# A weighted neighbour sum in a two-layer graph kernel: each partition holds eight list edges in a row, summed on VectorE for two destinations ahead of the one-hot products

## The chip, the cores and the metric

One Trainium2 chip; the kernel uses one of its cores. The metric is device time in microseconds of one execution. Ten executions of the kernel before gave a median of 6719.75 us (6715.77 to 6725.78). The profile and the trace come from one further execution.

## The reference, cut to what matters

6250 nodes with 256 features and 206,250 edges, sorted by destination (100,000 random pairs in both directions and a self-loop for each node; the sources are in random order). Two layers. The first is a graph attention and a routed FFN. The second is a weighted neighbour sum with two dense products and a dense mixture-of-experts FFN, gated by a second graph attention over another edge list:

```python
x = x + _L0_gnn_ref(_layernorm(x, axis=-1), edge_index, ...)
x = x + _L0_ffn_ref(_layernorm(x, axis=-1)[None], ...)[0]
x = x + _L1_gnn_ref(_layernorm(x, axis=-1), src, dst, edge_weight, L1_gnn_W1, L1_gnn_b1, L1_gnn_W2, L1_gnn_b2)
x = x + _L1_ffn_ref(_layernorm(x, axis=-1)[None], ...)[0]

def _L1_gnn_ref(embeddings, edge_src, edge_dst, edge_val, W1, b1, W2, b2):
    ego_emb = embeddings @ W1.T + b1
    messages = edge_val[:, None] * embeddings[edge_src]
    neighbor_emb = jax.ops.segment_sum(messages, edge_dst, num_segments=embeddings.shape[0])
    interaction_emb = neighbor_emb * embeddings
    side_emb = (neighbor_emb + interaction_emb) @ W2.T + b2
    out = ego_emb + side_emb
    out = jnp.where(out >= 0, out, LEAKY_SLOPE * out)
    norm = jnp.sqrt(jnp.sum(out * out, axis=1, keepdims=True))
    return out / jnp.maximum(norm, EPS)

# the second FFN, for each of its four experts
    g = jnp.where(topk_i == ei, w, 0.0).sum(-1)
    hh = jax.nn.gelu(x @ W1[ei] + b1[ei], approximate=False)
    out = out + g[..., None] * (hh @ W2[ei] + b2[ei])
```

The change is in the neighbour sum, `messages` and `segment_sum`.

## The kernel before, in words

The node features X stay in SBUF as 49 blocks of 128 nodes. The stages follow one another:

| stage | us in the trace | what it does |
|---|---|---|
| start | 0 to 97 | check of the edge list (check_stream, L982), list columns loaded and turned into the partitions (turn_rows, L1050) |
| layer 0 attention | 97 to 2250 | layer norm, projection, stream of the edges |
| layer 0 FFN (ffn0, L651) | 2250 to 3306 | routed FFN on TensorE in tiles; beside it a generator (sorted_edges, L1381) sorts the second edge list, a few steps per tile |
| gates, layer norm | 3306 to 3401 | the outputs of the routed FFN are gated (L631), the table tab_ef of normalised rows is written |
| neighbour sum ("n1f", L1793) | 3402 to 5644 | the stage that the change rewrites |
| layer 1 attention and gating (layer1_fast) | 5644 to 6718 | stream of the second edge list; y of the experts is read, gated and added (put, L1656) |

The neighbour sum goes over the edges in 202 pieces of Q = 8 columns of 128 edges. A column of 128 edges lies across the partitions: partition p of column j holds edge (8q + j) x 128 + p of the list. For each piece
- GpSimd issues eight indirect DMAs (gather, L233), each of which fetches the 128 source rows of a column from tab_ef into g1 (five buffers);
- ScalarE multiplies each column by its edge weights (L1921);
- VectorE compares the destinations of the columns with an iota and so makes eight one-hot matrices of 128x128 (one_hots, L1092);
- TensorE multiplies each one-hot by its column (L1901; one f32 product shows as two matmul records) and adds up in PSUM, in acc. An acc stands for a window of 128 destinations and takes two pieces (16 columns).

VectorE copies a finished acc to SBUF (kept, L1906). The window is then moved onto the block of 128 nodes that it belongs to by a shift product (move, L1827). When a block's sum is whole, a chain of steps follows, one per iteration: side (L1832), dense (L1841), norm (L1852), next_ln (L1861) and next_h (L1866), which ends with the input of the second FFN for the block. When four blocks are there, start (in dense_ffn) puts the work items of their expert FFN in a list: inner (L1560: matmuls, then the gelu on ScalarE, L1565) and outer (L1571: matmuls, then the addition of the bias b2 on VectorE, L1576, and a store of y to DRAM). A call of beside() issues the matmuls of one item, and the gelu or addition of the item before it. What is left when the pieces are over is issued in a loop at the end.

The order on each engine is written out by hand (manual_schedule): in iteration s_ the gathers of piece s_ are issued, then the products of piece s_ - 3 with three calls of beside() between them, then the steps of the chain, then the scalings and one-hots of piece s_ - 2. Each engine takes its own instructions in this order.

A list is taken by this fast path if a check finds that each column's destinations lie within its window (flag, in check_stream); else a general path runs.

Of the kernel before, what the change touches and what calls it, by code (L numbers as in the profile page):

```python
# [10 lines left out]

# [8 lines left out]
F32 = mybir.dt.float32  # L20
# [50 lines left out]
def tile_kernel(ctx, tc, src_ins, out):  # L71
# [841 lines left out]


    class Stream:
# [8 lines left out]
        def __init__(self, name, edges, slack, nodes, group=None):  # L924
# [57 lines left out]
    def check_stream(s, dst, flag, last_d, dl_d, psum=None, lend=None):  # L982
# [4 lines left out]
        with ExitStack() as held:  # L987
# [34 lines left out]
            nc.sync.dma_start(last_d, t)  # L1022

# [21 lines left out]
            nc.vector.tensor_reduce(bad, v, AX.XY, OP.add)  # L1045
            ps = pp.tile([P, 4, P], F32, name="pt_s")[:, 0, 0:1]
# [26 lines left out]
    Q = 8  # L1073
# [430 lines left out]

    def layer1_weights(lp):
# [16 lines left out]
    def dense_ffn(e_pool, fp, fpp, y_d):  # L1522
# [12 lines left out]
        b2 = e_pool.tile([P, E1, D], F32, name="b2")  # L1535
        nc.scalar.dma_start(b2, I["L1_ffn_b2"][None].to_broadcast([P, E1, D]))
# [31 lines left out]
        def outer(g, e, j):  # L1568
# [22 lines left out]
    def layer1_fast(s1, si1, dl1, il1, ha_d, tab_1, y_d):  # L1591
# [3 lines left out]
        with tc.tile_pool(name="g1f", bufs=1) as g1, tc.tile_pool(name="f1w", bufs=2) as fp:  # L1595
# [12 lines left out]
            nc.vector.scalar_tensor_tensor(own, own, 0.2, own, op0=OP.mult, op1=OP.max)  # L1608
            vec = g1.tile([P, 3, D1], F32, name="vec")
# [46 lines left out]
            def put(gates, j, b):  # L1656
                y = ys.pop(b)
                for e in range(E1):
                    nc.vector.scalar_tensor_tensor(X[:, b, :], y[:, e, :], gates[:, j, e:e + 1], X[:, b, :],
                                                   op0=OP.mult, op1=OP.add)  # L1660
# [20 lines left out]
    def fast(flag_s0, last_d, dl_d):  # L1681
# [7 lines left out]
        si = kp.tile([P, C * P], I32, name="si")  # L1689
        dl = kp.tile([P, C * P], F32, name="dl")  # L1690
        wt_d = dram.tile([P, C * P], F32, name="wt_d")
        tab = dram.tile([NP, D + H0], F32, name="tab")
        with tc.tile_pool(name="gat0f", bufs=1) as g0:
            il = g0.tile([P, C * P], F32, name="il")
            NI = g0.tile([P, NT, 2 * H0], F32, name="NI")
            with tc.tile_pool(name="rows", bufs=1) as p:
# [83 lines left out]
        with tc.tile_pool(name="sort", bufs=1) as sp, tc.tile_pool(name="sort_ps", bufs=1, space=PSUM) as pp:  # L1780
            ffn0(sorted_edges(s1, sp, pp, si1, dl1, il1, flag1))
# [11 lines left out]
        with tc.tile_pool(name="n1f", bufs=1) as ep, tc.tile_pool(name="n1fw", bufs=2) as mp, \  # L1793
                tc.tile_pool(name="n1f_ps", bufs=1, space=PSUM) as pp, \
                tc.tile_pool(name="f1_ps", bufs=2, space=PSUM) as fpp:
            wt = ep.tile([P, C * P], F32, name="wt")
            nc.sync.dma_start(wt, wt_d)
# [11 lines left out]
            acc, piece, hots, ems, sums_of = {}, {}, {}, {}, {}  # L1809
            T = s0.T  # L1810
            npiece = -(-T // Q)
            stages = {}

            def span(q):
# [163 lines left out]
```

## Time and profile before

| | us |
|---|---|
| median of 10 runs | 6719.75 |
| profiled execution | 6719.51 |
| its span | 6717.7 |

Busy time of the engines in the span, and in the neighbour sum (3402 to 5500, from the first gather to the last):

| engine | whole span, us | share | 3402 to 5500, us |
|---|---|---|---|
| TensorE matmul (PE) | 4323.3 | 64% | 1711.0 |
| VectorE (DVE) | 3120.9 | 46% | 479.6 |
| ScalarE (ACT) | 1545.3 | 23% | 998.3 |
| GpSimd (POOL) | 4083.4 | 61% | 1527.2 |

The mean granted TensorE clock over the span is 0.794 of full speed. The page also shows the span in 40 slices: a digit is the busy share in tenths, PEclk is the granted clock in tenths, and DMA is the mean busy share of the 16 DMA engines.

```
PE   4466666666666569999647888888888885111111
DVE  5355555555555781443332222222222222677777
ACT  2000000000000112322124544444444441000000
POOL 0677777777777112232157777667666752777774
PEclk9677777777777679999868999999999997555555
DMA  4544554454454135556553444334333431232222
```

A slice is 168 us, so the neighbour sum is slices 21 to 33. There TensorE is the busiest, GpSimd the next, and VectorE is idle most of the time. In a row of instruction groups the columns are: line, engine, operation, output and inputs, tile shapes, count, then busy time and mean duration in ns, then the idle time before them and what ended it. In a timeline row they are: start, duration, engine, line, operation, names, shapes, count, and in brackets the idle time before it with what ended that. "issue" is time in which the engine waited for nothing that the profile shows. L12 is line 12 of the kernel.

### The profile page before, as it was taken

How to read it: one execution, taken by the hardware profiler on the slowest of the kernel's cores; microseconds unless marked ns; L12 is line 12 of the kernel's file. 1: busy time of each engine (PE TensorE's matmuls, PEld its weight loads, DVE VectorE, ACT ScalarE, POOL GpSimd, SP SyncE). 2: the span in 40 equal slices, each digit the busy share in tenths (PEclk: the TensorE clock that was granted, in tenths of full speed). 3: DMA queues.
4: the chain of work that ended last, by engine and by line, in shares of the span. 5: the costliest groups of instructions: out<-in, count | busy, mean ns of one | idle time of the engine just before them, and what ended most of it. 6: DMA issues, size and time to landing. Idle time of an engine off the chain costs nothing.

```text
span 6717.7 us, 63729 instructions
## 1 busy us (share of the span) xinstructions
PE 4323.3 (64%) x19844; PEld 3330.4 (50%) x19844; DVE 3120.9 (46%) x7430; ACT 1545.3 (23%) x3735; POOL 4083.4 (61%) x4308
## 2 busy tenths in 40 slices
PE   4466666666666569999647888888888885111111
PEld 3344444444444448888525666666666664111111
DVE  5355555555555781443332222222222222677777
ACT  2000000000000112322124544444444441000000
POOL 0677777777777112232157777667666752777774
PEclk9677777777777679999868999999999997555555
DMA  4544554454454135556553444334333431232222
GB/s 137 141 139 137 139 139 137 139 139 137 138 140 137 57 91 192 186 188 224 164 156 112 119 121 119 113 112 121 113 113 113 119 91 50 61 70 69 67 67 59
DMA packets 502118, 817.25 MB, mean 122 GB/s; under 512 B 149515, under 2 KB 322983, under 8 KB 501738
## 3 DMA queue, kind: packets, MB, share of 16 engines
q0 software_dynamic: 190688, 461.74, 25.3%
q1 hardware_dynamic: 298414, 339.67, 16.3%
q10 hardware_dynamic: 12668, 11.68, 0.6%
q8 instruction: 160, 2.62, 0.2%
q14 instruction: 188, 1.54, 0.1%
HBM read 739.86 MB, written 76.05 MB: 121 GB/s over the span
## 4 chain that ended last, share of the span: by engine, by line
PE 38%; POOL 19%; DVE 16%; issue 12%; DMA 11%; ACT 3%; DVEq 0%; SPq 0%; another core or an unknown queue 0%; POOLq 0%; ACTq 0%
POOL g L1199 16%; PE acc L1901 10%; DMA g<-tab,si 7%; PE pf L1571 5%; PE pf L1560 5%; PE ph L600 5%; PE py L613 5%; DVE oh L1092 3%; PE acc L1301 3%; DMA g<-tab_1f,si1s 2%; POOL g L233 2%; DVE g L1278 1%; PE bacc L1827 1%; PE pt L262 1%; PE ph L1738 1%
## 5 line engine op out<-in xcount | busy, mean ns | idle before, releaser
L233 POOL DMA_INDIRECT g<-tab_ef,si x1612 | 1527.2, 947 | 665.0 <-issue 553.6
L1199 POOL DMA_INDIRECT g<-tab,si x1612 | 1539.5, 955 | 492.6 <-issue 410.6
L1301 PE MATMUL acc<-g,oh 128*128 128x264 f32 x3224 | 1049.7, 491 | 332.4 <-DVE g L1278 327.4
L1901 PE MATMUL acc<-g,oh 128*128 128x256 f32 x3224 | 885.9, 418 | 422.5 <-DVE oh L1092 223.1
L1301 PEld LDWEIGHTS acc<-g,oh 128*128 128x128 f32 x3224 | 776.6, 249 | 555.3 <-DVE g L1278 387.1
L1901 PEld LDWEIGHTS acc<-g,oh 128*128 128x128 f32 x3224 | 653.0, 209 | 650.8 <-ACT g L1921 373.1
L1199 POOL DMA_INDIRECT g<-tab_1f,si1s x787 | 765.2, 972 | 247.0 <-issue 216.3
L1921 ACT ACTIVATE g<-g,wt 128x256 f32<-128x256 f32 x1612 | 676.1, 496 | 150.0 <-DMA g<-tab_ef,si 149.0
L1092 DVE TENSOR_TENSOR oh<-ips,dl 128x1024 f32<-128x1024 f32 x404 | 489.1, 1212 | 0.0
L1278 DVE TENSOR_TENSOR g<-g,pe 128x2048 f32<-128x2048 f32 (+2 forms) x301 | 487.1, 1618 | 0.0
L1301 PE MATMUL acc<-s,oh 128*128 128x72 bf16 x1267 | 96.6, 251 | 548.8 <-DVE s L1283 548.8
L1231 DVE TENSOR_TENSOR z<-g,nd 128x32 f32<-128x32 f32 (+1 forms) x301 | 59.0, 196 | 815.4 <-DMA g<-tab,si 643.4
L600 PE MATMUL ph<-xe,w 128*128 128x256 f32 x1792 | 401.2, 381 | 0.0
L1571 PE MATMUL pf<-w,h 128*128 128x256 f32 x1568 | 399.3, 402 | 0.0
L613 PE MATMUL py<-w,h 128*128 128x256 f32 x1792 | 399.2, 381 | 0.0
L1560 PE MATMUL pf<-xt,w 128*128 128x512 f32 (+1 forms) x832 | 398.3, 607 | 0.6
L576 POOL DMA_INDIRECT xg<-tab_x,gi x112 | 123.8, 1106 | 398.3 <-PE pt L585 313.4
L1301 PEld LDWEIGHTS <-oh 128*128 128x128 bf16 x1267 | 90.1, 133 | 552.6 <-issue 477.4
L600 PEld LDWEIGHTS ph<-xe,w 128*128 128x128 f32 x1792 | 340.0, 191 | 45.4
L613 PEld LDWEIGHTS py<-w,h 128*128 128x128 f32 x1792 | 337.1, 191 | 43.4
L1220 PEld LDWEIGHTS <-ot 128*128 128x128 bf16 x2879 | 116.0, 101 | 474.8 <-DVE ot L1209 422.1
L1571 PEld LDWEIGHTS pf<-w,h 128*128 128x128 f32 x1568 | 318.8, 204 | 51.2 <-issue 1.9
(461 smaller groups left out, 5062.9 us busy)
## 6 DMA issues: line engine op xcount, KB each, us to landing
w<-in_L_ffn_W SPq DMA_DIRECT2D x112, 1024.0 KB
db<-s_d SPq DMA_DIRECT2D x299, 256.0 KB
g<-tab,si POOLq DMA_INDIRECT x1612, 2.8
g<-tab_ef,si POOLq DMA_INDIRECT x1612, 2.8
y_d<-y SPq DMA_DIRECT2D x196, 128.0 KB
yb<-y_d SPq DMA_DIRECT2D x49, 512.0 KB
g<-tab_1f,si1s POOLq DMA_INDIRECT x787, 2.3
yy<-tab_y SPq DMA_DIRECT2D x7, 1792.0 KB
```

The costliest lines, as they stand in the source:

```text
L233: nc.gpsimd.indirect_dma_start(out=dst, out_offset=None, in_=table, in_offset=bass.IndirectOffsetOnAxis(ap=si[:, t:t + 1], axis=0))
L576: nc.gpsimd.indirect_dma_start(out=xg[:, i, :], out_offset=None, in_=tab_x, in_offset=bass.IndirectOffsetOnAxis(ap=gi[:, 2 * j + i:2 * j + ...
L600: nc.tensor.matmul(ph, w1[:, k, f * P:(f + 1) * P], xe[:, k, :], start=(k == 0), stop=(k == KD - 1))
L613: nc.tensor.matmul(py, hs[f][:, i * P:(i + 1) * P], w2[:, f, :], start=(f == 0), stop=(f == FC - 1))
L1092: nc.vector.tensor_tensor(o[:, :m], ips[:, None, k * P:(k + 1) * P].to_broadcast([P, m, P]), dl[:, a:a + m, None].to_broadcast([P, m, P]), ...
L1199: nc.gpsimd.indirect_dma_start(out=g[:, j, :DH + H], out_offset=None, in_=tab, in_offset=bass.IndirectOffsetOnAxis(ap=si[:, t0 + j:t0 + j ...
L1278: nc.vector.tensor_mul(gh, gh, ps[i][:, o:o + n, :, None].to_broadcast([P, n, H, CD]))
L1301: nc.tensor.matmul(acc[b].rearrange("p s w -> p (s w)"), oh[:, t - a], m_, start=(t == lo), stop=(t == hi))
L1560: nc.tensor.matmul(ph[:, :n], w1[:, e, k, f * P:(f + 1) * P], xts[g][:, k, :n], start=(k == 0), stop=(k == KD - 1))
L1571: nc.tensor.matmul(py[:, :D], hs[g, e, f][:, j * P:(j + 1) * P], w2[:, e, f, :], start=(f == 0), stop=(f == FC - 1))
L1901: nc.tensor.matmul(acc[b], oh[:, t - a], g[:, t - t0, :], start=(t == lo), stop=(t == hi))
L1921: nc.scalar.activation(piece[k][:, j, :], piece[k][:, j, :], AF.Copy, scale=wt[:, t0 + j:t0 + j + 1])
```

## The change

1. *Order of the list.* Partition p of column j of piece q holds edge (128q + p) x 8 + j: eight edges that follow one another in the list lie in one partition. Since the list is sorted, and each node has at least 15 edges, eight edges in a row have one destination or two. The check of the list gets a further condition (at most one change of destination in eight).
2. *Sums on VectorE.* Per piece the eight gathered columns are added in each partition into two sums r[0] and r[1], one for each destination of the row, with the edge weight as a scalar per partition, which is zero where the edge belongs to the other destination: two scaled copies on ScalarE and 13 multiply-and-add operations on VectorE. One comparison makes two one-hots in place of eight, and two products (four matmul records) take the place of eight (16).
3. *Lists in DRAM.* The sources, the two masked weights and the two destinations per row in the new order are made by a new generator, runs_of, which runs in ffn0 after sorted_edges, and are loaded at the beginning of the neighbour sum (si 832 KB, wab 1.65 MB, dab). The load, turn and store of the edge weights at the start of the kernel fall away, and the load of wt.
4. *Other moves.* kept is copied by ScalarE. The bias b2 is no longer added in outer (ScalarE copies y from PSUM); put in layer 1 adds it with the gates, in eight operations per block instead of four. The three calls of beside() stand before the products, after them and after the sums.

```diff
+            if s.two:
+                turns = p.tile([P, C, P // Q], F32, name="turns")
+                nc.vector.tensor_reduce(turns, ends_of.rearrange("p c (r j) -> p c r j", j=Q)[:, :, :, :Q - 1],
+                                        AX.X, OP.add)
...
+                nc.vector.tensor_add(bad, bad, over[:, 1:2])
...
+    def runs_of(s, sp, pp, si, wab, dab):
...
+        def load(dst, ap, c, nr):
+            full = min(nr, max(0, E // F - c * P))
+            if full < P:
+                nc.vector.memset(dst, 0.0)
+            nc.sync.dma_start(dst[:full], ap[c * P * F:(c * P + full) * F].rearrange("(r e) -> r e", e=F))
...
+        def turned(dst, src):
+            d, t = (a.rearrange("p (r j) -> p r j", j=Q) for a in (dst, src))
+            for j0 in range(0, Q, 4):
+                pt = pp.tile([P, 4, P], F32, name="pt_s")
+                for j in range(4):
+                    nc.tensor.transpose(pt[:, j], t[:, :, j0 + j], ident)
+                nc.scalar.copy(d[:, :, j0:j0 + 4].rearrange("p r j -> p j r"), pt)
+
+        for c in range(-(-npiece // P)):
...
+            load(a.bitcast(I32), I["src"], c, nr)
...
+            turned(y, b)
+            so = sp.tile([P, F], I32, name="so")
+            nc.vector.tensor_copy(so, y)
+            nc.sync.dma_start(si[:, cols], so[:, :nr * Q])
+            yield
...
+            for k, op in enumerate((OP.is_equal, OP.not_equal)):
+                m = room(("A1", "B1")[k])
+                nc.vector.tensor_tensor(m.rearrange("p (r j) -> p r j", j=Q), d3, first, op=op)
+                nc.vector.tensor_mul(m, m, wt)
+                nc.sync.dma_start(wab[k, :, cols], m[:, :nr * Q])
+                yield
...
             def put():
                 y = fp.tile([P, D], F32, name="y1", bufs=2)
-                nc.vector.tensor_add(y, py[:, :D], b2[:, e])
+                nc.scalar.copy(y, py[:, :D])
                 nc.sync.dma_start(y_d[g * GB + j, :, e, :], y)
...
                 for e in range(E1):
-                    nc.vector.scalar_tensor_tensor(X[:, b, :], y[:, e, :], gates[:, j, e:e + 1], X[:, b, :],
-                                                   op0=OP.mult, op1=OP.add)
+                    for v in (y, b2):
+                        nc.vector.scalar_tensor_tensor(X[:, b, :], v[:, e, :], gates[:, j, e:e + 1], X[:, b, :],
+                                                       op0=OP.mult, op1=OP.add)
...
-                wr = load_rows(p, I["edge_weight"], s0.edges, C, F32, "wr")
-                wT = p.tile([P, C * P], F32, name="wT")
-                turn_rows(wT, wr, C)
-                nc.sync.dma_start(wt_d, wT)
...
-            ffn0(sorted_edges(s1, sp, pp, si1, dl1, il1, flag1))
+            ffn0(itertools.chain(sorted_edges(s1, sp, pp, si1, dl1, il1, flag1),
+                                 runs_of(s0, sp, pp, si_d, wab_d, dab_d)))
...
-            wt = ep.tile([P, C * P], F32, name="wt")
-            nc.sync.dma_start(wt, wt_d)
+            si = ep.tile([P, npiece * Q], I32, name="si8")
+            nc.sync.dma_start(si, si_d)
+            wab = ep.tile([P, 2, npiece * Q], F32, name="wab")
+            nc.sync.dma_start(wab, wab_d.rearrange("k p t -> p k t"))
+            dab = ep.tile([P, npiece * 2], F32, name="dab")
+            nc.sync.dma_start(dab, dab_d)
...
+            def sum_runs(q):
+
+                g = piece.pop(q)
+                r = [mp.tile([P, D], F32, name=f"run{i}", bufs=3) for i in range(2)]
+                for j in range(Q):
+                    for i in range(min(2, j + 1)):
+                        w = wab[:, i, q * Q + j:q * Q + j + 1]
+                        if j == i:
+                            nc.scalar.activation(r[i], g[:, j, :], AF.Copy, scale=w)
+                        else:
+                            nc.vector.scalar_tensor_tensor(r[i], g[:, j, :], w, r[i], op0=OP.mult, op1=OP.add)
+                oh = mp.tile([P, 2, P], F32, name="oh", bufs=3)
+                nc.vector.tensor_tensor(oh, ips[:, None, :P].to_broadcast([P, 2, P]),
+                                        dab[:, 2 * q:2 * q + 2, None].to_broadcast([P, 2, P]), op=OP.is_equal)
+                runs[q] = r, oh
...
-                        for j in range(n):
-                            gather(g[:, j, :], tab_e, si, t0 + j)
+                        for j in range(Q):
+                            gather(g[:, j, :], tab_e, si, s_ * Q + j)
+                    beside()
                     q = s_ - 3
                     if 0 <= q < npiece:
...
-                            for t in range(a, a + m):
-                                nc.tensor.matmul(acc[b], oh[:, t - a], g[:, t - t0, :], start=(t == lo), stop=(t == hi))
-                                if t - t0 in (1, 4, 7):
-                                    beside()
...
+                        r, oh = runs.pop(q)
+                        last = q % 2 == 1 or q == npiece - 1
+                        for k in range(2):
+                            nc.tensor.matmul(acc[i], oh[:, k], r[k], start=(q % 2 == 0 and k == 0), stop=(last and k == 1))
+                        if last:
+                            kept = mp.tile([P, D], F32, name="kept1", bufs=3)
+                            nc.scalar.copy(kept, acc.pop(i))
+                            after.setdefault(s_ + 1, []).append((move, i, (kept,)))
+                    beside()
                     for f, b, args in after.pop(s_, []):
...
-                        for j in range(n):
-                            nc.scalar.activation(piece[k][:, j, :], piece[k][:, j, :], AF.Copy,
-                                                 scale=wt[:, t0 + j:t0 + j + 1])
-                        hots[k] = one_hots(s0, k, mp, ips, dl, 3)
+                    if 0 <= s_ - 2 < npiece:
+                        sum_runs(s_ - 2)
+                    beside()
                     s_ += 1
```

The order of the instructions of the neighbour sum stays that of the code: in an iteration VectorE gets the steps of the chain first, then the 13 operations and the one-hot of piece s_ - 2. g1 keeps its five buffers; a buffer is free when the sum of its piece is done, where it was free after the products.

More of the change, by code (lines that the diff above doesn't have):

```diff
@@ L1022, in check_stream @@
             nc.sync.dma_start(last_d, t)
+            if s.two:
+                ends_of = t
+                t = p.tile(shape, F32, name="t2")
             at = p.tile(shape, F32, name="at")
@@ L1808, in fast @@
             ips = place_iota(pp)
[L1809 to L1814, printed above, removed]
-                return q * Q, min(Q, T - q * Q)
+            acc, piece, runs, ems, sums_of = {}, {}, {}, {}, {}
+            def sum_runs(q):
[12 more added lines that the diff above has]
+                runs[q] = r, oh
             def move(i, kept):
```

89 lines of the change are left out of this document (67 added, 22 removed).

## The prediction

> **What bounds the kernel now.** I read the page's chain of waits first, to see which engines make up the end, then its costliest groups, then windows and waits of the stretch that the change rewrites.
>
> ```profile
> PE 38%; POOL 19%; DVE 16%; issue 12%; DMA 11%; ACT 3%; DVEq 0%; SPq 0%; another core or an unknown queue 0%; POOLq 0%; ACTq 0%
> ...
> L233 POOL DMA_INDIRECT g<-tab_ef,si x1612 | 1527.2, 947 | 665.0 <-issue 553.6
> L1901 PE MATMUL acc<-g,oh 128*128 128x256 f32 x3224 | 885.9, 418 | 422.5 <-DVE oh L1092 223.1
> L1921 ACT ACTIVATE g<-g,wt 128x256 f32<-128x256 f32 x1612 | 676.1, 496 | 150.0 <-DMA g<-tab_ef,si 149.0
> L1092 DVE TENSOR_TENSOR oh<-ips,dl 128x1024 f32<-128x1024 f32 x404 | 489.1, 1212 | 0.0
> ```
>
> TensorE leads the chain over the whole program, but that share mixes stages. In this stage (3402 to 5644) the group of 3224 matmuls that the change cuts to 808 takes 886 us, so a reader may expect hundreds of microseconds. The next view, windows of the gathers of L233 (POOL's busy time and count, granted clock, DMA share, GB/s), says otherwise.
>
> ```profile
> 3700.00:3900.00 200.00, 151.33 (x160) 0.94 0.42 120
> 4300.00:4500.00 200.00, 139.72 (x149) 0.93 0.40 114
> 5100.00:5300.00 200.00, 140.80 (x150) 0.93 0.40 112
> ```
>
> 160 gathers in 200 us is one per 1.25 us: 0.95 of work and 0.30 of issue, GpSimd's own pace. Eight make a piece, so 10.0 us per piece is a floor that stays. At 149 or 150 the pace is 1.34. The waits between 3500 and 5500 tell what holds them (total us, times, longest):
>
> ```profile
> DVE on L1848 <- PE pt L1846: 459.6, 45, 14.5
> POOL g L233 <- issue: 435.4, 1426, 0.5
> DVE kept L1906 <- PE acc L1901: 410.1, 94, 9.4
> PE acc L1901 <- DVE oh L1092: 215.9, 130, 2.5
> POOL g L233 <- PE acc L1901: 76.9, 44, 5.0
> POOL g L233 <- ACT g L1921: 20.8, 19, 2.8
> ```
>
> Gathers wait for a buffer only 76.9 + 20.8 = 98 us. That is nearly all that lighter products can give here. The first gather starts at 3402.1 and the last ends at 5499.6: 2097 us against 202 x 10.0 = 2020. Behind lie 46 us to the last acc (5546), 24 to the last next_h (5570) and 74 of expert FFN on TensorE alone (to 5644); the last two stay.
>
> **What takes the place of TensorE.** Per piece VectorE now does one 1.21 us one-hot. After the change it does 13 scalar_tensor_tensor of 128x256 (two operands in SBUF) and a one-hot of a quarter the size. Their price, from the yy gates at L631, the same operation, shape and sources; beside it a chained form:
>
> ```profile
> 3330.90 5.24 DVE L631 SCALAR_TENSOR_TENSOR X<-yy,g,X 128x256 f32<-128x256 f32 x13
> ...
> 6054.40 4.01 DVE L1659 SCALAR_TENSOR_TENSOR X<-yb,r_gates,X 128x256 f32<-128x256 f32 x8
> 6054.63 1.07 POOL L1199 DMA_INDIRECT g<-tab_1f,si1s  x1 [0.30 <-issue]
> ```
>
> 5.24/13 = 0.40 each where the sums alternate; 0.50 where each reads the last one's result, as at L1659. The new sums alternate between r0 and r1: 5.24, plus 0.41 for the one-hot (1.21 at 1024 wide, 0.68 at 512 in the same helper, so 0.68 - 0.27 at 256) and 0.1 for ScalarE's start of the first sum = 5.75 per piece, 4.5 more than now. That fits in 10.0 by itself. But VectorE works in order, and each iteration's chain step comes ahead of the sum: it waits for TensorE, which waits for the previous one-hot. So there is a loop from one-hot to one-hot, and I cost each of its four kinds (work of the other engines from this stage's timeline):
> - move and dense: acc 4 x 0.275 = 1.10, a beside item 1.89, move 1.03, dense 2.06, two VectorE operations 0.85, sum 5.75: 12.7.
> - norm: acc 1.10, kept (now on ScalarE) 0.37, gelu 0.69, square 0.60, table load 1.28, root 0.20, VectorE 0.79, sum 5.75: 10.8.
> - next_ln: statistics 0.60, root 0.29 with a table load in half the cases (0.64), normalise 0.57, sum 5.75: 7.9.
> - side and next_h: acc 1.10, item 1.89, transposes to the copy of h 3.3, h 0.18, sum 5.75: 12.2.
>
> With a work item the four make 43.6. Without one the item, gelu and its table load fall out: 10.8 + 8.8 + 7.2 + 10.3 = 37.1. A group brings 34 items into about 16.5 pieces of three slots, so about 12 iterations of 16 have one: (3 x 43.6 + 37.1)/16 = 10.5 us per piece. TensorE also slows after idling: 16 matmuls after a wait took 5.38 us at 4149 against 3.69 when warm. The iterations without items hold some 8 us of matmuls on the loop in 16; at half to full extra they add 0.25 to 0.5 per piece. I take 10.7, bounds 10.1 (the queue overlaps more, gathers lead) and 11.2.
>
> The end of the stage: the first eight pieces go at the gathers' pace from a first gather at about 3410 and the last of them is summed near 3495; then 194 pieces, 20 us of chain and the 74 of FFN. 3495 + 194 x 10.7 + 94 = 5665, against 5644: **+21**. This holds the later first gather, which now waits for si (832 KB, read back through SP's queue beside 2 MB of w1; the first gathered rows already land only near 3427). Wab is 1.65 MB where wt was 0.83, also there before the first sum. Each 0.1 us per piece is 19 us; at 10.1 it is -96, at 11.2 +118.
>
> Removed without gain: 1612 ScalarE scalings become 404, 676 us that the loop leaves for kept copies (101 x 0.4) and y copies (196 x 0.4). The y add leaves VectorE, whose late puts would otherwise lie in the loop. The three beside calls move from between products to before the products, after them and after the sum; two of them run under VectorE's 5.75, the middle one is in my loop.
>
> **A rule against the change.** A gather beside the 8 operations above took 1.07 us, those after it 0.94; over all the gathers that began beside such operations the means are 1.01 and 0.98; the longest beside L1859, the same operation in this stage, is 1.20. The sort's 128x512 two-operand operations stretched one gather of L576 to 1.79. I take +0.02 on average, bounds 0 and +0.25, so that the gather floor stays under the loop. The Trainium skill (SBUF — State Buffer, section "SBUF: two separate sides") says that VectorE with two SBUF inputs and GpSimd take a shared port pair as an exclusive lock, the other waiting for the whole instruction. Taken fully, a piece would be 8 x 0.95 + 5.24 = 12.8, and this stage would be an estimated 430 us longer; the rows for this very shape show at most 4.2 x 0.25 = 1.05 of those 5.24 (4.2 gathers begin in 5.24 us at 1.25).
>
> **The other places.**
> - Start: the load, 13 transposes and store of edge weights go. VectorE began the first layer norm at 97.20 after 9.16 us that ended with the store wt_d; il was done at 89.85. **-6** (0 to -7). The new turns reduce lies in a 5.3 us DMA wait.
> - Beside ffn0: runs_of adds two chunks of loads, 12 groups of four transposes (0.60 each, 7.2), VectorE masks and stores. The queues it is moved into are SP's (the weight loads of the FFN are there) and GpSimd's (an iota). TensorE is the bound there. The sort's tail with like steps, 3083 to 3149, gave four tiles in 66.3 us against 4 x 14.25: +9.3 for half as many groups. **+19**, bounds +7 (the transposes alone) and +45 (rows of 4 KB that land late).
> - layer1_fast: put makes 8 operations for 4: 196 x 0.50 = 98 us of VectorE. Until 6655 GpSimd paces the stage (787 gathers, period 1.28) and VectorE is busy 746 of 1011, so 5 to 10 show; of the last 63 us VectorE is busy 48 and the extra puts of the last group and some backlog add 10 to 15. **+18**, bounds +5 and +40. Its b2 load shares the start with HN: in that number.
>
> Sum: -6 + 19 + 21 + 18 = +52. On the profiled run, span 6717.7 and whole 6719.51, that is **6771 us**; that run lies 0.24 under the median 6719.75, which changes nothing.
>
> **The rivals.**
> - *GpSimd sets the pace* (other side): the sums overlap the chain so well that the loop stays at 10.2 or less. For it: VectorE is busy only 116 us of the 500 from 4000, ScalarE 240, and buffers of five pieces let gathers lead. Against: the order on VectorE is fixed by hand and two of the four kinds cost over 12. At 10.2: 3495 + 1979 + 94 = 5568, -76; with the other +31, -45: 6674. It decides below 10.43, where the stage gives back 31.
> - *Port contention paces the gathers*: the same 4.2 gathers per piece; at +0.25 each a piece is 10.0 + 1.05 = 11.06, +91 in the stage, +35 elsewhere: 6845. For: 1.79 at L576. Against: 0.98 to 1.01 at L1659.
> - *The change doesn't run*: if a row of eight edges met three destinations, the flag would send the program to the general path. Every node has at least 15 incoming edges in a list sorted by destination, so eight neighbours meet two at most. 0.01 at most.
>
> **How the numbers follow.** The loop at 10.45 to 11 with sums as above: 0.55. GpSimd's pace: 0.28. Contention at +0.15 or more per gather: 0.16. The likeliest gives 6771, with its own range 6720 to 6835. The range that holds 8 in 10 reaches to the first rival's price and past the second's: 6674 to 6850. About 0.2% (13 us) is what a measurement can tell from no change; the loop's low end (10.4 to 10.5) lies within it. Faster is most of the first rival (0.24) and 0.03 of the loop, same 0.10 their border, slower the rest, 0.63.
>
> **What would show it.** In the profile after: the gathers of the stage idle for VectorE's sums (releaser DVE r), some 140 us in total (0.7 x 202), at 149 or 150 per 200 us throughout; VectorE busy 58% of the stage where it is 23% (480 of 2098, less 245 for the old one-hots, 42 for kept, 82 for the y adds, and 202 x 5.65 more), its idle time ended by TensorE's on and h; the new operations at 0.40; gathers near 0.95 to 0.98. ffn0 ends near 3319, the stage 21 longer, layer 1 at 1092 for 1074. I am wrong if gathers run at 160 per 200 us throughout (first rival), if their mean is over 1.05 (second), or if matmuls of the stage double in length throughout, for lack of work.

## The result, and the profile after

| | before | after |
|---|---|---|
| median, us | 6720.17 (28 runs) | 6831.31 (8 runs, 6816.55 to 6842.27) |
| ratio | | 1.0164 (95% interval 1.0155 to 1.0173) |
| span of the profiled run, us | 6717.7 | 6827.9 |

The kernel became slower by 111 us, where 52 was predicted. The two spans are cut at five marks: the first and last gather of each stage, the first load of yy behind the routed FFN, and the iota that opens layer 1.

| part | before | after | difference | predicted |
|---|---|---|---|---|
| start and layer 0 attention, to its last gather | 0 to 2213.2 | 0 to 2202.1 | -11.1 | -6 |
| routed FFN, to the first load of yy | to 3308.8 | to 3338.9 | +41.2 | +19 |
| gates and layer norm, to the first gather of the neighbour sum | to 3402.1 | to 3436.1 | +3.9 | in the next |
| first to last gather | 2096.5 | 2192.6 | +96.1 | |
| last gather to layer 1 | 145.4 | 101.5 | -43.9 | |
| neighbour sum, these three | | | +56.1 | +21 |
| layer 1 | 1073.7 | 1097.7 | +24.0 | +18 |
| sum | 6717.7 | 6827.9 | +110.2 | +52 |

The chain by engine from the page of after, then three rows of its list of groups, those of the neighbour sum (line numbers moved; L234 is the gather, L1922 the new sum, L2011 the products):

```profile
PE 26%; DVE 22%; POOL 20%; issue 15%; DMA 13%; ACT 4%; DVEq 0%; SPq 0%; another core or an unknown queue 0%; ACTq 0%; POOLq 0%
...
L234 POOL DMA_INDIRECT g<-tab_ef,si x1616 | 1701.7, 1053 | 590.6 <-issue 441.8 <-DMA si<-si_d 98.6 <-DVE run L1922 33.2
L1922 DVE SCALAR_TENSOR_TENSOR run<-g,wab,run 128x256 f32<-128x256 f32 x2626 | 1091.1, 479 | 113.9 <-DMA g<-tab_ef,si 80.5 <-ACT run L1920 25.9
...
L2011 PE MATMUL acc<-run,oh 128*128 128x256 f32 x808 | 334.2, 555 | 863.2 <-DVE oh L1924 863.2
```

The products did what was meant: 3224 matmul records and 886 us became 808 and 334. VectorE has 1091 us of sums, and 908 us more in all (4028.7 for 3120.9). The line to look at is the first: one gather takes 1053 ns, where it took 947. Over 1616 gathers that is 171 us. Windows of the gathers (POOL's busy time and count, clock, DMA share, GB/s):

```profile
3700.00:3900.00 200.00, 155.22 (x148) 0.77 0.40 111
4300.00:4500.00 200.00, 154.42 (x149) 0.80 0.41 115
5100.00:5300.00 200.00, 154.50 (x150) 0.76 0.40 112
```

The count is near the prediction's 149 or 150, but POOL is busy 155 us of 200, where before it was 140 to 151. The rest is issue, 0.30 each: the waits of POOL alone, 3500 to 5500 (total us, times, longest), show no wait longer than that.

```profile
POOL g L234 <- issue: 403.4, 1324, 0.3
POOL g L234 <- DVE run L1922: 30.5, 100, 0.3
POOL g L234 <- ACT run L1920: 2.7, 9, 0.3
```

So no gather waits for a buffer any more; the 98 us of such waits before are gone (the 98.6 for si in the row above stand before the first gather). GpSimd never rests, and its gathers are longer. The timeline shows when (start, duration, engine, line):

```profile
4227.77 2.85 DVE L1922 SCALAR_TENSOR_TENSOR run<-g,wab,run 128x256 f32<-128x256 f32 x7
4228.57 2.86 POOL L234 DMA_INDIRECT g<-tab_ef,si  x1 [0.30 <-issue]
...
4302.74 0.94 POOL L234 DMA_INDIRECT g<-tab_ef,si  x1 [0.30 <-issue]
4303.29 5.38 DVE L1922 SCALAR_TENSOR_TENSOR run<-g,wab,run 128x256 f32<-128x256 f32 x13
4303.98 1.12 POOL L234 DMA_INDIRECT g<-tab_ef,si  x1 [0.30 <-issue]
4305.41 0.94 POOL L234 DMA_INDIRECT g<-tab_ef,si  x1 [0.30 <-issue]
4306.66 1.22 POOL L234 DMA_INDIRECT g<-tab_ef,si  x1 [0.30 <-issue]
```

A gather that begins inside a run of VectorE's sums may take 0.94, 1.12, 1.22 or 2.86 us; the one of 2.86 began 2.05 us before the run of sums ended and came to its end 0.81 after it. Most long ones end so: of the 61 gathers of over 1.5 us between 3500 and 5630, 54 end 0.81 to 0.83 us behind the last sum of a run. Of the 1568 gathers in that stretch, put by the operation of VectorE that they overlap most, the 853 beside L1922 have a mean of 1.143 and hold 167.9 us over 0.946; the 499 beside no operation have 0.946 and hold nothing over it.

In the routed FFN the tiles, by the first gather of each, lie 14.25 us apart without list work. Three tiles beside runs_of took 21.35, 35.95 and 26.81 where the kernel before had 14.26, 14.25 and 14.25. The load, VectorE, GpSimd's store of y and TensorE in the second of them:

```profile
3165.54 0.30 SPq L1535 DMA_DIRECT2D A<-in_src  x1
...
3182.05 0.69 DVE L1553 CAST A<-A 128x1024 f32<-128x1024 int32 x1 [14.21 <-DMA A<-in_src]
3182.66 0.42 DVE L616 TENSOR_TENSOR y<-py,bb 128x256 f32<-128x256 f32 x1
...
3183.36 1.21 POOL L617 DMA_INDIRECT tab_y<-y,so  x1 [14.02 <-DVE y L616]
...
3186.90 1.09 PE L1545 MATMUL pt_s<-ident,A 128*128 128x128 f32 x4 [11.89 <-DVE A L1556]
```

The load of the second chunk's sources needs 16.5 us to land. VectorE waits for it 14.2 us, and the FFN's own addition (y at L616) stands behind it. TensorE in its turn waits 11.9 us for VectorE at the list's transposes, and the FFN's matmuls stand behind those.

In six of the eight sessions of the runs that follow the kernel before took about 16% longer (7766 to 7856 us), and every profile taken there shows some 2900 to 3600 us of waits, added up over the engines, for something outside the core ("remote"), where the others show none; these runs are called "disturbed" here, and their times are compared only with each other.

### The profile page after: what moved, and what is told of

It is laid out like the page before. It is cut to its first block, busy times and chain, and to the rows that moved or that the text cites. A ratio compares the mean times of both kernels' runs of the same rounds, so it can differ in the third digit from the quotient of the medians.

```text
span 6827.9 us, 61938 instructions
## 1 busy us (share of the span) xinstructions
PE 3942.0 (58%) x17463; PEld 2942.5 (43%) x17463; DVE 4028.7 (59%) x9984; ACT 1166.9 (17%) x2834; POOL 4264.6 (62%) x4320
## 4 chain that ended last, share of the span: by engine, by line
PE 26%; DVE 22%; POOL 20%; issue 15%; DMA 13%; ACT 4%; DVEq 0%; SPq 0%; another core or an unknown queue 0%; ACTq 0%; POOLq 0%
POOL g L1214 15%; DVE run L1922 8%; DMA g<-tab,si 7%; PE py L614 5%; PE ph L601 5%; POOL g L234 4%; PE acc L2011 4%; PE acc L1316 3%; PE pf L1654 2%; DMA g<-tab_1f,si1s 2%; DVE X L1756 2%; DMA g<-tab_ef,si 2%; PE pf L1665 2%; DVE g L1293 1%; PE pt L263 1%
## 5 line engine op out<-in xcount | busy, mean ns | idle before, releaser
L234 POOL DMA_INDIRECT g<-tab_ef,si x1616 | 1701.7, 1053 | 590.6 <-issue 441.8
L1922 DVE SCALAR_TENSOR_TENSOR run<-g,wab,run 128x256 f32<-128x256 f32 x2626 | 1091.1, 479 | 113.9 <-DMA g<-tab_ef,si 80.5
L1316 PEld LDWEIGHTS acc<-g,oh 128*128 128x128 f32 x3224 | 775.3, 248 | 558.9 <-DVE g L1293 392.5
L2011 PE MATMUL acc<-run,oh 128*128 128x256 f32 x808 | 334.2, 555 | 863.2 <-DVE oh L1924 863.2
L2011 PEld LDWEIGHTS acc<-run,oh 128*128 128x128 f32 x808 | 193.5, 263 | 999.5 <-DVE oh L1924 841.2
L1654 PE MATMUL pf<-xt,w 128*128 128x512 f32 (+1 forms) x832 | 435.5, 665 | 1.2 <-ACT h L1659 1.0
L1665 PE MATMUL pf<-w,h 128*128 128x256 f32 x1568 | 414.4, 418 | 10.3 <-ACT h L1659 10.3
L1665 PEld LDWEIGHTS pf<-w,h 128*128 128x128 f32 x1568 | 335.4, 215 | 86.0 <-issue 16.0
L617 POOL DMA_INDIRECT tab_y<-y,so x112 | 118.6, 1058 | 292.8 <-DVE y L616 288.6
```

What stands on the lines that cost most here:

```text
L234: nc.gpsimd.indirect_dma_start(out=dst, out_offset=None, in_=table, in_offset=bass.IndirectOffsetOnAxis(ap=si[:, t:t + 1], axis=0))
L1316: nc.tensor.matmul(acc[b].rearrange("p s w -> p (s w)"), oh[:, t - a], m_, start=(t == lo), stop=(t == hi))
L1654: nc.tensor.matmul(ph[:, :n], w1[:, e, k, f * P:(f + 1) * P], xts[g][:, k, :n], start=(k == 0), stop=(k == KD - 1))
L1665: nc.tensor.matmul(py[:, :D], hs[g, e, f][:, j * P:(j + 1) * P], w2[:, e, f, :], start=(f == 0), stop=(f == FC - 1))
L1922: nc.vector.scalar_tensor_tensor(r[i], g[:, j, :], w, r[i], op0=OP.mult, op1=OP.add)
L2011: nc.tensor.matmul(acc[i], oh[:, k], r[k], start=(q % 2 == 0 and k == 0), stop=(last and k == 1))
```

## The experiments

Theory A: gathers are stretched by VectorE operations with two SBUF operands, and gathers set the pace. Theory B, the prediction's: the loop through VectorE's fixed order sets it. Theory C: both stand at nearly the same height.

**The sums in PSUM.**

```diff
+                u = pp.tile([P, 2, D], F32, name="runp")
...
-                            nc.scalar.activation(r[i], g[:, j, :], AF.Copy, scale=w)
+                            nc.scalar.activation(u[:, i], g[:, j, :], AF.Copy, scale=w)
...
-                            nc.vector.scalar_tensor_tensor(r[i], g[:, j, :], w, r[i], op0=OP.mult, op1=OP.add)
+                            nc.vector.scalar_tensor_tensor(r[i] if j == Q - 1 else u[:, i], g[:, j, :], w, u[:, i],
+                                                           op0=OP.mult, op1=OP.add)
...
-                nc.vector.tensor_tensor(oh, ips[:, None, :P].to_broadcast([P, 2, P]),
-                                        dab[:, 2 * q:2 * q + 2, None].to_broadcast([P, 2, P]), op=OP.is_equal)
+                for k in range(2):
+                    nc.vector.tensor_scalar(oh[:, k], iota, dab[:, 2 * q + k:2 * q + k + 1], None, op0=OP.is_equal)
```

> The two running sums stand in PSUM instead of SBUF (only the last of each is written to SBUF, for TensorE), so that none of the 13 VectorE operations reads two operands from SBUF; the one-hot becomes two comparisons with a scalar for each partition. The number of VectorE operations on the sums is the same. Theory A (gathers are stretched by VectorE operations with two SBUF operands, and the gathers set the pace): the mean gather falls from 1.053 us to about 0.95, the 167 us of stretch go, and the neighbour sum becomes shorter by 60 to 165 us, depending on what comes next; whole about 6670 to 6770. Theory B (the prediction's: the loop through VectorE's fixed order sets the pace, the longer gathers only fill idle time): gathers fall to 0.95 too, but then wait for buffers as much as they gained; the stage stays within 20 us, whole 6810 to 6850.

> The two running sums in PSUM, as in the run e1_psum, to be read on a chip whose DMA is not disturbed (the kernel before near 6720). Theory A (gathers are stretched by VectorE operations with two SBUF operands, and the gathers set the pace): the mean gather falls from 1.053 us to about 0.95 and the neighbour sum becomes shorter by 60 to 165 us; whole about 6670 to 6770. Theory B (the loop through VectorE's fixed order sets the pace): gathers fall to 0.95 too, but then wait for buffers as much as they gained; the stage stays within 20 us, whole 6810 to 6850.

e1_psum was disturbed (8263.38 beside 7855.81). e5_psum took 7106.59 beside 6719.00. Its groups:

```profile
L234 POOL DMA_INDIRECT g<-tab_ef,si x1616 | 1529.2, 946 | 992.5 <-issue 745.3
...
L1922 DVE SCALAR_TENSOR_TENSOR runp<-g,wab,runp 128x256 f32<-128x256 f32 x2222 | 1086.5, 489 | 199.0 <-ACT runp L1920 131.6
```

The gather is back at 946, in both runs, and they have the list in the new order too, so the order isn't what stretched it. But the time missed both expectations, the nearer one by 257 us: back to back an operation on PSUM takes 0.52 us (ten in 5.21), where the change's take 0.41 (13 in 5.38), and ScalarE's products wait 493 us for VectorE's sums, argued to be through the shared tile. From first to last gather the run took 2421.9 us, 11.99 for a piece, and gathers wait for buffers again (120 us for ScalarE's products alone). So the stretch goes with the place of the operand, and with longer operations the loop through VectorE does become the limit, at 12, well above the gathers.

**The sum ahead of the chain.**

```diff
+                    if 0 <= s_ - 2 < npiece:
+                        sum_runs(s_ - 2)
                     for f, b, args in after.pop(s_, []):
...
-                    if 0 <= s_ - 2 < npiece:
-                        sum_runs(s_ - 2)
                     beside()
```

> On VectorE and ScalarE the sum of a piece is issued ahead of the chain's steps of the same iteration, not behind them, so that it no longer waits for TensorE; nothing else changes. Theory A (stretched gathers set the pace): the gathers' mean stays at 1.04 to 1.07 and the stage within 15 us, whole 6815 to 6845. Theory B (the loop from one-hot to one-hot sets the pace): the loop shortens to the sums and the chain's own operations, below 8 us for a piece, and the stage by 60 us or more, whole below 6770.

> The sum of a piece ahead of the chain's steps on VectorE and ScalarE, as in the run e4_sumfirst, to be read on a chip whose DMA is not disturbed. Theory A (stretched gathers set the pace): the gathers' mean stays at 1.04 to 1.07 and the stage within 15 us, whole 6815 to 6845. Theory B (the loop from one-hot to one-hot sets the pace): the stage shortens by 60 us or more, whole below 6770.

e4_sumfirst was disturbed (8004.47 beside 7855.81). e6_sumfirst took 6785.69 beside 6719.00, between the two expectations. Its gathers:

```profile
L234 POOL DMA_INDIRECT g<-tab_ef,si x1616 | 1654.4, 1024 | 590.2 <-issue 447.2
```

They still wait for no buffer, so they set the pace. Their mean fell to 1024, below what A had said. In sum they are 47.3 us shorter than in the changed kernel, and from first to last gather the run is 47.1 us shorter (2145.5 for 2192.6): what the gathers lose is what the stage gains. Why this order stretches them less is only argued: more of them lie beside sums (950 for 853), but with a mean of 1.074, and VectorE's sums are broken up there by 488 us of waits for ScalarE's first products.

**One SBUF operand instead of two.** The additions are left out here.

```diff
-                            nc.vector.scalar_tensor_tensor(r[i], g[:, j, :], w, r[i], op0=OP.mult, op1=OP.add)
+                            nc.vector.tensor_scalar(r[i], g[:, j, :], w, None, op0=OP.mult)
```

> The 13 operations per piece multiply a gathered column by its weight and write it to the sum's tile, without reading the sum (one SBUF operand; the additions are left out, so the output isn't the reference's). Place, count and length (about 0.41 us) of VectorE's operations stay. Theory A (the stretch alone is what the stage lost): gathers at 0.95, period 1.25 to 1.28, first to last gather 2020 to 2070 us instead of 2193, whole 6670 to 6720. Theory C (the loop stands right behind): gathers at 0.95 with waits for buffers, period 1.31 to 1.36, whole 6780 to 6830.

> The kernel of e13_one_operand again (13 operations per piece with one SBUF operand; the additions are left out, so the output isn't the reference's), for a chip on which the kernel before takes about 6720. Theory A (the stretch alone is what the stage lost): gathers at 0.95, period 1.25 to 1.28, first to last gather 2020 to 2070 us instead of 2193, whole 6670 to 6720. Theory C (the loop stands right behind): gathers at 0.95 with waits for buffers, period 1.31 to 1.36, whole 6780 to 6830.

> The kernel of e13_one_operand again (13 operations per piece with one SBUF operand; the additions are left out, so the output isn't the reference's). On a chip on which the kernel before takes about 6720: Theory A (the stretch alone is what the stage lost): gathers at 0.95, period 1.25 to 1.28, first to last gather 2020 to 2070 us instead of 2193, whole 6670 to 6720. Theory C (the loop stands right behind): gathers at 0.95 with waits for buffers, period 1.31 to 1.36, whole 6780 to 6830.

e13_one_operand and e15_one_operand were disturbed (8032.65 beside 7765.9, 8021.96 beside 7773.04). e16_one_operand took 6674.31 beside 6718.84, as A had said. Its groups, then the same windows as above:

```profile
L234 POOL DMA_INDIRECT g<-tab_ef,si x1616 | 1540.0, 953 | 590.9 <-issue 444.2
...
L1922 DVE TENSOR_SCALAR run<-g,wab 128x256 f32<-128x256 f32 x2626 | 849.4, 383 | 195.8 <-DMA g<-tab_ef,si 162.5
```

```profile
3700.00:3900.00 200.00, 151.52 (x160) 0.83 0.42 120
4300.00:4500.00 200.00, 151.54 (x160) 0.78 0.43 120
5100.00:5300.00 200.00, 151.52 (x160) 0.80 0.43 121
```

160 gathers in every window: GpSimd's free pace. The gathers are 161.7 us shorter in sum than in the changed kernel, the stage from first to last gather 161.3 (2031.3). One doubt is left: this operation takes 0.28 us back to back (13 in 3.62), not the 0.41 that was expected, so VectorE's loop was shorter by 1.8 us per piece too.

**A control for that doubt.** The operation and its length stay; it adds a constant tile in PSUM, and the sums are left out.

```diff
-                            nc.vector.scalar_tensor_tensor(r[i], g[:, j, :], w, r[i], op0=OP.mult, op1=OP.add)
+                            nc.vector.scalar_tensor_tensor(r[i], g[:, j, :], w, ips, op0=OP.mult, op1=OP.add)
```

> The 13 multiply-and-add operations per piece stay, at the same place, but add a constant tile that lies in PSUM instead of the sum in SBUF (so one SBUF operand each; the sums themselves are left out, so the output isn't the reference's). By rows of e5_psum such an operation (PSUM in, SBUF out) takes 0.43 us, where the change's take 0.41. Theory A (the stretch alone is what the stage lost): period 1.25 to 1.28, no waits for buffers, first to last gather 2020 to 2070 us, whole 6670 to 6725 (on a chip where the kernel before takes about 6720). Theory C (the loop stands right behind): waits for buffers, period 1.30 to 1.36, whole 6760 to 6830.

The run was disturbed (8211.97 beside 7854.26), and its time doesn't settle the doubt: from first to last gather it took 2756.3 us, e13_one_operand and e15_one_operand 2621.5 and 2613.7, all longer than the 2507.3 of e2_spread (a disturbed run below, with the sums as in the change). The gathers don't set the pace in these runs: between 4000 and 6100 GpSimd is busy 1147 us of 2100 in e17_control and 1224 in e15_one_operand. The durations tell more:

```profile
L234 POOL DMA_INDIRECT g<-tab_ef,si x1616 | 1528.5, 946 | 1327.0 <-issue 1047.5
...
L1922 DVE SCALAR_TENSOR_TENSOR run<-g,wab,ips 128x256 f32<-128x256 f32 x2626 | 1066.5, 476 | 76.0 <-issue 27.0
```

Same operation, same count, 476 ns for 479, and no stretch. From 3850 us on 563 gathers lie beside these operations, with a mean of 0.947; in e2_spread 666 lie beside the change's, with 1.324. The sums' chain is gone here as well, but e5_psum keeps it, in PSUM, and has no stretch either. So the second operand in SBUF makes it. Over all 18 runs, disturbed or not, the mean gather is 1024 to 1105 with two SBUF operands in the sum (5 runs) and 946 to 953 with one (13 runs).

**The loop without the stretch.** The same PSUM sums, with ScalarE's first products issued together ahead of VectorE's operations (up); with the sum ahead of the chain as well (up_first); and with the first products made by VectorE (dve_first):

```diff
-                            nc.scalar.activation(u[:, i], g[:, j, :], AF.Copy, scale=w)
+                            nc.vector.tensor_scalar(u[:, i], g[:, j, :], w, None, op0=OP.mult)
```

> As e5_psum (running sums in PSUM), but ScalarE's two first products are issued together ahead of VectorE's operations, so that the second no longer waits for VectorE's first (in e5_psum that wait, through one shared tile, was 371 us). Theory C (two limits of nearly the same height: gathers stretched by VectorE at 10.85 us for a piece, and right behind them the loop through VectorE's fixed order, which the prediction put at 10.5 to 11): gathers at 0.95 with waits for buffers, a mean period of 1.30 to 1.38, whole 6780 to 6860. Theory A (the stretched gathers alone cost the time, the loop is well below 10 us for a piece): period at most 1.28, whole below 6740.

> Both at once: running sums in PSUM with ScalarE's first products together, and the sum ahead of the chain's steps on VectorE and ScalarE. Theory C: with the stretch and the loop both taken away the gathers run at their own pace, mean period 1.25 to 1.28, first to last gather 2020 to 2070 us instead of 2193, whole 6670 to 6720. Theory D (something else holds the stage, such as ScalarE's order or TensorE at a low clock): period at 1.30 or more, whole 6750 or more.

> As e8_psum_up_first, but the two first products are made by VectorE itself (15 operations in place of 13), so that the sum waits for ScalarE no more. Theory C: the same as e8_psum_up_first within 15 us, since the gathers pace both. If ScalarE's order is the limit there (theory D), this one is faster than e8_psum_up_first by 20 us or more.

> The kernel of e7_psum_up again (running sums in PSUM, ScalarE's two first products together), for a chip on which the kernel before takes about 6720. Theory C (two limits of nearly the same height: stretched gathers at 10.85 us for a piece, and right behind them the loop through VectorE's fixed order, 10.5 to 11): gathers at 0.95 with waits for buffers, a mean period of 1.30 to 1.38, whole 6780 to 6860. Theory A (the stretched gathers alone cost the time): period at most 1.28, whole below 6740.

> The kernel of e9_psum_dve_first again (running sums in PSUM, VectorE makes the two first products itself, the sum ahead of the chain's steps), for such a chip. Theory C: with the stretch and the loop both taken away the gathers run at their own pace, period 1.25 to 1.28, first to last gather 2020 to 2070 us instead of 2193, whole 6670 to 6720. Theory D (something else holds the stage, such as TensorE at a low clock): period at 1.30 or more, whole 6750 or more.

All five were disturbed: 8101.68, 8239.15 and 7987.71 beside 7774.24, then 8119.50 and 7985.08 beside 7775.42. The gathers took 946 to 949 in each. e9_psum_dve_first took 251 us less than e8_psum_up_first, which has theory D's sign. The times repeat within 0.3%, but say nothing of an undisturbed run. So it stays open how fast sums in PSUM can be made.

**The list loads a tile ahead.**

```diff
             load(a.bitcast(I32), I["src"], c, nr)
+            for _ in range(5):
+                yield
...
             nc.sync.dma_start(a[:nr].bitcast(I32), s.dpad[P + c * P * F:P + (c * P + nr) * F].rearrange("(r e) -> r e", e=F))
+            for _ in range(5):
+                yield
             nc.vector.tensor_copy(b, a.bitcast(I32))
...
             load(w, I["edge_weight"], c, nr)
+            for _ in range(5):
+                yield
```

> Beside the routed FFN the lists in the new order are made as before, but each load is issued more than a tile (five steps) ahead of its first use. Theory A (the FFN's 41 us are waits: VectorE and TensorE take their instructions in order, and the FFN's own stand behind list operations that wait for loads of up to 16 us): the FFN shortens by 25 to 35 us, whole about 6800. Theory B (the 41 us are the work itself, 12 groups of transposes, copies and masks, and its DMA traffic beside the weight loads): within 8 us of no change, whole 6820 to 6835.

Disturbed (7925.88 beside 7855.81), but the FFN's length can be compared with its neighbours on the same chip. From the last gather of layer 0 to the first load of yy it took 1112.8 us, against 1151.1, 1150.3 and 1146.4 in e1_psum, e3_b2back and e4_sumfirst, which leave the lists as in the change: 34 to 38 less. (The three runs below that have these loads too took 1114 to 1117.) Theory A of this run holds there: the larger part of the FFN's 41 us were waits for loads, put in front of the FFN's own instructions.

**b2 back in the expert FFN.**

```diff
-                nc.scalar.copy(y, py[:, :D])
+                nc.vector.tensor_add(y, py[:, :D], b2[:, e])
...
-                    for v in (y, b2):
-                        nc.vector.scalar_tensor_tensor(X[:, b, :], v[:, e, :], gates[:, j, e:e + 1], X[:, b, :],
-                                                       op0=OP.mult, op1=OP.add)
+                    nc.vector.scalar_tensor_tensor(X[:, b, :], y[:, e, :], gates[:, j, e:e + 1], X[:, b, :],
+                                                   op0=OP.mult, op1=OP.add)
```

> The bias b2 is added again by VectorE in the expert FFN's y (the kernel before's form), and layer 1 adds four products per block, not eight. Theory A (gathers pace the neighbour sum, so 196 VectorE additions of 0.42 us with one SBUF operand there cost nothing): layer 1 goes from 1098 back to about 1074, the neighbour sum stays within 10 us, whole about 6805. Theory B (VectorE's loop paces the neighbour sum): layer 1 gains the same 24, but the neighbour sum grows by 30 to 80 us, whole 6835 to 6890.

Disturbed (7972.58 beside 7855.81): layer 1 took 1422.7 us against 1525.0 in e2_spread, and first to last gather 2612.5 against 2507.3. The signs are B's, but the run is inconclusive for an undisturbed chip, where the changed kernel's gathers left VectorE idle 41% of the stage.

**Parts together.** e14_parts joins the list loads, b2 back and the sum ahead of the chain, with sums in SBUF; e12_all joins them with dve_first; e18_best is e12_all with one comparison for both one-hots.

> The changed kernel with three parts altered: loads of the lists more than a tile ahead beside the routed FFN, b2 added by VectorE in the expert FFN again, the sum ahead of the chain's steps; sums in SBUF as in the change. If they add up: 38 less in the FFN (by e2_spread), 24 less in layer 1, 46 less in the neighbour sum (by e6_sumfirst), with up to 10 back for the additions on VectorE: whole 6715 to 6740, level with the kernel before. If the additions cost as much as they save: 6750 or more.

> As e11_psum_dve_first, with the loads of the lists more than a tile ahead beside the routed FFN (as e2_spread) and b2 added by VectorE in the expert FFN again (as e3_b2back). If the parts add up: 25 to 40 less in the routed FFN and 24 less in layer 1 than e11_psum_dve_first, at most 20 more in the neighbour sum; whole 6600 to 6670 where that one is near 6690, below the kernel before. If VectorE is full in the neighbour sum, the 196 additions of 0.42 us (82 us) come back there in part.

> Sums in PSUM, VectorE makes its two first products itself, one comparison for both one-hots from an iota in SBUF, the sum ahead of the chain's steps, list loads more than a tile ahead in the routed FFN, b2 in the expert FFN again. VectorE's work per piece is 9.2 us (2 x 0.48, 11 x 0.52, 2 x 0.44, 0.41, chain 0.83, b2 0.41), just under the gathers' 10.0. If the order lets it run nearly without gaps: gathers at 1.25 to 1.30, whole 6600 to 6690, below the kernel before. If gaps add more than 1.2 us per piece, VectorE is the bound: period 1.38 or more, whole 6780 or more.

All disturbed. e14_parts took 7763.51 (8 runs) beside 7765.90 (9 runs), ratio 1.0006 (0.9984 to 1.0028): level with the kernel before, as expected. e12_all took 1.0159 (1.0124 to 1.0193) and e18_best 1.0125 (1.0080 to 1.0170) of the kernel before; whether they gain on an undisturbed chip, as their expectations held possible, stays open. No version with the whole sum was faster than the kernel before.

## Why the prediction was wrong

- *What bounds the kernel before.* Right: GpSimd's 10.0 us per piece was the floor, and lighter products could give back no more than the 98 us of waits for buffers. They did: those waits are gone.
- *The step that failed* is "I take +0.02 on average, bounds 0 and +0.25, so that the gather floor stays under the loop". The gathers beside the sums took 1.143, +0.197 each; over all it was +0.107, 8 x 0.107 = 0.86 us per piece, and the floor rose to 10.85 (2192.6/202), above the loop. I had taken the price from rows where VectorE ran four or eight such operations now and then; here there are 13 for every eight gathers. The bound of +0.25 held, and the rival built on it (6845, chance 0.16) names what happened (6831). That its number is so near is partly luck: it put +91 on the stage, where +56 came, and +35 elsewhere, where +54 came.
- *A sign that was read short.* The prediction has one gather of L576 stretched to 1.79. The trace of the kernel before has nine of about 1.78 and one of 2.25, beside five operations on two SBUF operands, back to back, of which this is the last:

```profile
2989.46 2.25 POOL L576 DMA_INDIRECT xg<-tab_x,gi  x1 [0.30 <-issue]
2990.45 0.42 DVE L1468 TENSOR_TENSOR B<-B 128x256 f32<-128x256 f32 x1
```

  It ended 0.84 us behind that operation, as the long ones of the changed kernel do. And the 21 gathers of this stage that began during an operation of L1859 have a mean of 1.057 (the 63 of L1659 1.00), where the prediction gives 1.01 and 0.98.
- *The loop at 10.7* was not the limit. The sums even waited for gathered rows (80.5 us, ScalarE's first products 170.6). Between 3650 and 5500 these waits are 64.1 and 115.7 us over some 170 pieces, 0.4 to 1.1 us each, so the loop lies at about 9.8 to 10.5: an estimate, and how much of the 161 us of e16_one_operand would come back at the change's own length of operations stays open, since e17_control was disturbed. That 10.7 stood near 10.85 was chance; the difference of 0.15 times 194 pieces is 29 of the 35 us by which the stage was missed. The 94 us put behind the last sum fit: the last gather is followed by 101.5.
- *The FFN's +19* was mis-sized: 41.2, inside its bounds of 7 and 45. I scaled the sort's tail by its number of steps; what counted was that loads of 16.5 us stood ahead of the FFN's instructions on VectorE.
- *Layer 1's +18* was 24: 17 us behind the last gather (62.3 to 79.3; 10 to 15 were said), the rest on the way. *The start's -6* was -9.6 at the first gather and -11.1 at the end of that stage.
- *What would show it.* The 140 us of waits for VectorE's sums didn't appear; VectorE's 59% (1242 us of 2098) did, for 58 foretold (the prediction's own terms add up to 1252, which is 60%); the mean of the gathers, over 1.05, was the sign given for the second rival.
- *The rule weighed.* The Trainium skill (SBUF — State Buffer, section "SBUF: two separate sides") has VectorE with two SBUF inputs and a GpSimd operation that reads SBUF lock each other out: the one that starts first keeps the shared ports for its whole instruction. Its kind is what these runs show: two operands stretch a gather (1053), one doesn't (946 in e17_control). Its full price, 12.8 us per piece, isn't: 10.85.

## What to carry to other kernels

When work moves to an idle engine, price what it does to the engine that sets the pace, in its own instructions' durations, not only the busy time of the engine that receives it. On GpSimd's side, compare the mean duration of a gather with and without VectorE's new operations: a stage that shows no waits at all can still be slower. List preparation that runs beside another stage should issue its loads a whole step of that stage before their first use, because an in-order engine that waits for them holds back everything behind.

## What the runs showed of the hardware

- The stretch comes in steps: of the 1568 gathers of the changed kernel most are at 0.95, then at 1.2 to 1.3 (254), 1.65 to 1.7 (28), 2.05 (7) and 2.85 (24). From 1.25 up the steps are about 0.4, as long as one VectorE operation (0.41), and nearly all of the long ones end 0.82 us behind the last sum of a run, as if they had waited for it. In e16_one_operand the longest was 1.21.
- A multiply of 128x256 with one SBUF operand and a scalar per partition takes 0.28 us back to back, a multiply-and-add 0.41 with its sum in SBUF and 0.52 with its sum in PSUM.
- With fewer products TensorE's granted clock in the stage fell from 0.93 or 0.94 to between 0.76 and 0.80 (the windows above), and a product's record rose from 418 to 555 ns.
